# An attention and feed-forward block on one core: the first twelve tiles laid out in a new order, with finer order words

## The chip, the cores and the metric

The kernel runs on one core of a Trainium2 chip. The core has a matrix engine (PE, with its weight loads shown apart as PEld), a vector engine (DVE), a scalar engine (ACT), a general engine (POOL) and a sync engine (SP) whose queue issues every DMA of this kernel. Each engine works through its own queue in order. The metric is the device time in microseconds of one launch; the time before is 529.81 us, the median of three runs (529.16 to 530.25).

## The reference, cut to what matters

```python
# x: (4, 2048, 512), ctx: (4, 154, 512), 16 heads of 64
out = attention(layernorm(x), ctx)         # 154 keys; key j is allowed for row i when j == i
x = x + out @ Wout + bout
h = layernorm(layernorm(x)) * gamma + beta
h = qlinear(h, w1, b1); h = gelu(h); h = qlinear(h, w2, b2)
x = x + h
def qlinear(x, w, b):      # whole-number weights in -1..1, rows scaled to 127
    scale = 127 / clip(max|x| of the row, EPS); xq = round(x * scale)
    sw = 1 / clip(mean|w|, EPS);                wq = clip(round(w * sw), -1, 1)
    return xq @ wq / (scale * sw) + b
```

The first 154 rows of a batch see one key each, so their softmax is 1 and they get the projection of the key of the same number. All later rows have no allowed key, so their softmax is even and they get the mean of the 154 projected keys. So the attention is a product of the context with W = Wv Wout (the value half of Wkv), and a few added rows: the first tile of 128 rows of a batch adds 128 products, the second one adds 26 products and the mean, all others the mean alone.

## The kernel before, in words

The 8192 rows are 64 tiles of 128 rows. `seq` (L72) starts each batch with its third tile, so that the first tiles need the mean of the keys alone. Tiles are normalised in groups of 1, 1, 1, 1, 2, 2, 2, 3, 3 and then 4 (L73).

The order of the whole program is written out by hand: the scheduler is switched off, `BEGINNING` holds one word for each operation up to step U11, `STEADY` is repeated for every four tiles from tile 12 on, and `ENDING` covers the last eight. A word is a letter, a tile number and sometimes a half or an engine flag (last digit 1 for DVE, 0 for ACT or POOL). What counts for the time is how the words fall into the five queues: within one engine they keep the order of the words.

Words for the beginning: `lv`, `lo` load 128 rows of Wv and Wout, `lw i.c` loads a chunk of weight i (0 for w1, 1 for w2, eight chunks of 512 KB each), `lc` the context, `lr` a row vector spread to 128 partitions (0 bout, 1 gamma, 2 beta, 3 b2), `lb` half of b1, `L` two tiles of x. `w` adds one block to W in PSUM, `cw` copies a quarter of W out. `ms` sums |w| of a chunk, `z` makes the weight scale from the eight sums, `q` scales and rounds a chunk to int16, `c` clips it to the final f16 weight. `sk`, `mk`, `lk`, `sf` prepare key sums and means. `pm` is the product for the mean of the first batch, `pr` the one for the rest rows, `Y b` the one for the first 128 keys of batch b; `m`, `yr`, `y b` take them out of PSUM with bout added; `sr` stores the rest rows to DRAM, `s` and `t` read them back spread out.

Words for a tile: `A`/`a` add the attention rows (DVE/POOL), `S` statistics, then one of three normalisations: `O P C E` on DVE with one power on POOL (C needs the power; E needs beta), `N` with `B` (ACT normalises, POOL multiplies gamma and adds beta) or `N` with `K` (POOL does all). `R` finds the row scale, `V`/`v` the group scales, `Q` quantises (ACT), `T` transposes by DMA, `I n.h` writes b1 into a PSUM half (the seed), `U` is the up product (16 matmuls), `G` the gelu of a half, `M` the maximum of a half, `H` quantises the hidden rows, `h` transposes them by DMA, `D` is the dequantisation factor, `W` the down product, `X` adds b2, `F` finishes, `f` stores.

Resources that set the order around the change: the ring of 12 buffers for x and staged weights (a load after the twelfth waits for the release of a buffer, in the order of the words); four buffers `wi` for whole-number chunks; three PSUM pairs of banks `ps_h` (W takes two, the products of batches 0 and 1 the third; after that every half of every tile takes the one that a gelu released three halves earlier); two banks `ps_o` for the remaining products; and eight DMA semaphores used in turn, so that a DMA's issue waits for the landing of the one issued eight before it.

Lines that matter later: L203 product of ones for the weight scale, L211 and L214 quantise and clip weights, L225 absolute sum on ACT, L237 add rows, L313 the normalised row with beta (word E), L316 add b2, L336 and L338 group scales, L391 blocks of W, L402 and L404 copies of W, L420 attention products, L502/L500 seeds on ACT/DVE, L510 up, L529 gelu, L541 maximum, L563 factor D, L570 quantise hidden, L588 down, L594 finish.

Of the kernel before, what the change touches and what calls it, by code (L numbers as in the profile page):

```python
# [53 lines left out]
def xattn_ffn(ctx: ExitStack, tc, x, ctxT, WvT, Wout, bout, w1T, b1, w2T, b2, gamma, beta, out):  # L54
# [22 lines left out]
    for g, size in enumerate(sizes):  # L77
# [19 lines left out]
        G2.1 X1 S7 a8 W0 N6 R5 H1 t1 h1 M2.1 P6 V4 D2 Q4 H2 E6 T4 B7 a9
        U3 h2 a11 R6 G3.0 X2 D1 Q5 I4.0.1 S8 a10 M3.0 F0 f0 R7 T5 S9 I4.1.0 L7 G3.1 M3.1
        P8 N8
        U4 H3 a13 X3 I5.0.1 B9 L8 W1 h3 E8 S10 F1 R8 v6 G4.0 I5.1.0 f1 S11 W2 a16  # L100
        U5 G4.1 Q6 s0 I6.0.0 M4.0 G5.0 M4.1 T6 a12 F2 f2 R9 D4 H4 M5.0 h4 S12 I6.1.0 G5.1
        X4 a17 D3 M5.1 W3
        U6 L9 A14 X5 N10 F3 f3 Q7 I7.0.1 S16 a15 W4 G6.0 I7.1.0 K10 Q8 T7
        U7 H5 S17 M6.0 V8 T8 B11 a18 G6.1 S13 B12 h5 S14 Q9 M6.1 I8.0.0 D5 G7.0 I8.1.0 T9
        S15 N13 M7.0 H6 R10 G7.1 D6 K13 W5 h6 X7 R11 F4 F5 a19 f4 L10 X6
        U8 W6 I9.0.1 G8.0 M7.1 I9.1.0 R12 V10 K14 M8.0 G8.1 M8.1 f5 H7 h7 S18 Q10
        U9 I10.0.1 S19 a20 H8 G9.0 I10.1.0 G9.1 T10 M9.0 R13 F6 W7 h8 f6 Q11 M9.1 D7 L11
        B15 S20 R14 T11 P16 D8
        U10 X9 H9 G10.0 I11.0.1 M10.0 N16 h9 I11.1.0 Q12 a21 R15 F7 W8 X8
        U11 f7 G10.1 I12.0.0 a22 G11.0 M10.1 K17 D9 L12 F8 T12 H10 D10 X10 V13 S21 h10  # L110
        G11.1 I12.1.0 E16 W9 K18 M11.0 R16 a23 X11 M11.1 t2 f8 R17 F9 Q13 S22 H11 T13 h11
        f9
# [83 lines left out]
    def weight_scale(i, step=None):  # L196
        if step != 1:
            tot[i] = small.tile([P, 1], F32, tag="tot", name=f"tot_{i}")
            nc.vector.tensor_reduce(tot[i], part[i], AX.X, ALU.add)
        if step == 0:  # L200
            return
        pt = ps_o.tile([P, 512], F32, tag="po", name=f"pt_{i}")
        nc.tensor.matmul(pt[:, 0:1], ones, tot[i], start=True, stop=True)  # L203
        nc.vector.tensor_scalar(wm[i], pt[:, 0:1], 1.0 / (D * HID), EPS, ALU.mult, ALU.max)
        nc.vector.reciprocal(sw[i], wm[i])
# [523 lines left out]
```

## Time and profile before

| What | Value |
|---|---|
| median of three runs | 529.81 us |
| the profiled execution: time / span of its trace | 528.89 us / 527.1 us |
| mean granted TensorE clock | 0.992 |
| PE busy | 498.8 us, 95% of the span |
| DVE, ACT, POOL busy | 434.8, 422.4, 405.4 us |
| up products (1024 matmuls), down products (1024) | 233.5 us, 231.2 us |
| PE idle ahead of up / down products | 13.4 us / 6.0 us |
| first block of W starts / first up product starts | 4.24 us / 53.58 us |

The span is measured from the first to the last instruction of the trace, and the time adds what lies around it (1.8 us here). A matmul's recorded length contains its pipeline, so 16 matmuls that follow each other take less than 16 times the mean of one: the timeline shows one up or down product in 3.45 us. An attention product of four f32 matmuls is recorded as eight and also takes 3.45 us. DMA times are read as the time of landing. "Idle before" names what ended the wait.

### The profile page before, as it was taken

To read this page: it belongs to the slowest core of one execution; us is meant where nothing else is said; L and a number is where in the kernel's file an instruction comes from. 1 tells how busy PE (TensorE), PEld (TensorE's weight loads), DVE (VectorE), ACT (ScalarE), POOL (GpSimd) and SP (SyncE) were. 2 spreads that over 40 slices of the span, in tenths; PEclk is the share of its full clock that TensorE was granted. 3 is DMA by queue.
4 is the path that set the end of the run, shared out by engine and by line. 5 is a ranking of instruction groups with operands and counts; after the bars stand their busy time and mean duration, and the time that the engine had idled before them with its cause. 6 is when DMAs were issued, how large, how long until landed. Compare 5 with 4: busy or idle time off the path is not lost.

```text
span 527.1 us, 6898 instructions
## 1 busy us (share of the span) xinstructions
PE 498.8 (95%) x2164; PEld 222.3 (42%) x2164; DVE 434.8 (82%) x760; ACT 422.4 (80%) x387; POOL 405.4 (77%) x526
## 2 busy tenths in 40 slices
PE   6999848998999999999999999999999999999996
PEld 2444313433444444444444444444444444444442
DVE  1078998998888898989899988999999998787762
ACT  1386876698789888898888879898888888888971
POOL 0045489999999999999999999899999998852220
PEclk9999979999999999999999999999999999999999
DMA  8998066675799797868777696858596956576654
GB/s 305 401 391 304 11 174 134 182 175 141 165 188 202 140 213 157 204 156 187 164 188 167 139 234 145 193 127 206 133 207 139 218 103 158 111 168 132 130 116 125
DMA packets 194112, 94.00 MB, mean 178 GB/s; under 512 B 170268, under 2 KB 170268, under 8 KB 194076
## 3 DMA queue, kind: packets, MB, share of 16 engines
q1 hardware_dynamic: 194076, 93.56, 73.6%
q8 instruction: 17, 0.28, 0.2%
q14 instruction: 19, 0.16, 0.1%
HBM read 34.55 MB, written 17.04 MB: 98 GB/s over the span
## 4 chain that ended last, share of the span: by engine, by line
PE 57%; POOL 16%; DVE 11%; DMA 9%; ACT 3%; issue 3%; SPq 0%; ACTq 0%; POOLq 0%; DVEq 0%
PE ph L510 28%; PE po L588 27%; POOL x L237 4%; DMA xqT<-xqg 3%; DVE m L541 3%; POOL h L300 2%; POOL h L299 2%; POOL x L316 2%; DMA ctx_sb<-ctxT_dram 2%; DVE bn L244 2%; DVE ph L500 1%; DMA ws<-w2T_dram 1%; PE wps L391 1%; DVE o L594 1%; POOL r L261 1%
## 5 line engine op out<-in xcount | busy, mean ns | idle before, releaser
L510 PE MATMUL ph<-w1q,xqT 128*128 128x512 f16 x1024 | 233.5, 381 | 13.4 <-DMA xqT<-xqg 10.0
L588 PE MATMUL po<-w2q,hqT 128*128 128x512 f16 x1024 | 231.2, 379 | 6.0 <-DMA hqT<-hq 6.0
L541 DVE TENSOR_REDUCE m<-hid 128x1 f32<-128x1024 f32 (+1 forms) x130 | 152.9, 1192 | 20.4 <-ACT hid L529 19.9
L529 ACT ACTIVATE hid<-ph,d 128x1024 f32<-128x1024 f32 (+1 forms) x130 | 141.1, 1093 | 24.1 <-PE ph L510 23.2
L570 ACT ACTIVATE hq<-hid,i 128x2048 f16<-128x2048 f32 (+1 forms) x65 | 128.2, 1974 | 39.0 <-issue 19.2
L510 PEld LDWEIGHTS <-xqT 128*128 128x128 f16 x1024 | 99.9, 98 | 138.7 <-DMA xqT<-xqg 15.2
L588 PEld LDWEIGHTS <-hqT 128*128 128x128 f16 x1024 | 99.7, 98 | 128.3 <-DMA hqT<-hq 8.9
L502 ACT ACTIVATE ph<-b_b,inv 128x1024 f32<-128x1024 f32 x81 | 89.9, 1112 | 4.4 <-POOL inv L336 3.4
L316 POOL TENSOR_TENSOR x<-x,b_b 128x512 f32<-128x512 f32 x63 | 80.2, 1283 | 0.0
L299 POOL TENSOR_TENSOR h<-h,gamma_b 128x512 f32<-128x512 f32 x56 | 71.6, 1278 | 5.4 <-ACT h L287 1.2
L300 POOL TENSOR_TENSOR h<-h,beta_b 128x512 f32<-128x512 f32 x56 | 71.4, 1274 | 4.4
L237 POOL TENSOR_TENSOR x<-x,mean 128x512 f32<-128x512 f32 x55 | 69.7, 1275 | 2.8 <-DMA x<-x_dram 2.8
L594 DVE SCALAR_TENSOR_TENSOR o<-po,d,x 128x512 f32<-128x512 f32 x64 | 47.8, 746 | 16.9 <-PE po L588 8.9
L500 DVE TENSOR_SCALAR ph<-b_b,inv 128x1024 f32<-128x1024 f32 x47 | 59.6, 1268 | 1.4 <-POOL inv L336 1.3
L322 DVE TENSOR_REDUCE m<-h 128x1 f32<-128x512 f32 x64 | 43.1, 675 | 6.7 <-POOL h L300 6.6
L342 ACT ACTIVATE xqg<-h,s 128x512 f16<-128x512 f32 x64 | 45.5, 711 | 1.6 <-DVE s L330 1.6
L244 DVE BATCH_NORM_STATS2 bn<-x 128x6 f32<-128x512 f32 x64 | 43.6, 682 | 2.5 <-POOL x L237 2.4
L563 POOL TENSOR_TENSOR d<-mh,wm 128x1 f32<-128x1 f32 x64 | 12.1, 198 | 39.8 <-DVE mh L556 35.9
L294 POOL TENSOR_SCALAR h<-x,rstd,shift 128x512 f32<-128x512 f32 x50 | 38.6, 773 | 0.0
L391 PE MATMUL wps<-wo,wv 128*128 128x512 f32 x64 | 30.9, 645 | 4.2 <-DMA wo<-Wout_dram 4.2
L214 POOL TENSOR_SCALAR w1q<-wi 128x1024 f16<-128x1024 int16 x6 | 6.1, 1035 | 31.8 <-ACT wi L211 31.8
L225 ACT ACTIVATE junk<-ws 128x1024 int16<-128x1024 f32 x10 | 10.5, 1051 | 19.3 <-DMA ws<-w1T_dram 17.9
(74 smaller groups left out, 251.7 us busy)
## 6 DMA issues: line engine op xcount, KB each, us to landing
x<-x_dram SPq DMA_DIRECT2D x32, 512.0 KB, 4.9
out_dram<-o SPq DMA_DIRECT2D x64, 256.0 KB, 2.8
ws<-w1T_dram SPq DMA_DIRECT2D x8, 512.0 KB, 7.2
ws<-w2T_dram SPq DMA_DIRECT2D x8, 512.0 KB
wv<-WvT_dram SPq DMA_DIRECT2D x8, 256.0 KB, 5.9
...
hqT<-hq SPq DMA_TRANSPOSE x65, 4.3
```

The source lines that it names most:

```text
L237: e.tensor_tensor(x_of(n), x_of(n), y, ALU.add)
L244: nc.vector.bn_stats(st, x_of(n))
L299: nc.gpsimd.tensor_tensor(normed[n], normed[n], gamma_b, ALU.mult)
L300: nc.gpsimd.tensor_tensor(normed[n], normed[n], beta_b, ALU.add)
L316: e.tensor_tensor(x_of(n), x_of(n), b2_b, ALU.add)
L500: nc.vector.tensor_scalar(ph, row, d, None, ALU.mult)
L502: nc.scalar.activation(ph, row, AF.Identity, bias=0.0, scale=d)
L510: nc.tensor.matmul(bank[i], xqT[n][:, k, :], w1q[:, k, i * 512 : (i + 1) * 512], start=False, stop=(k == KD - 1), skip_group_check=True,)
L529: nc.scalar.activation(hidden[n][:, i * w : (i + 1) * w], up_ps[n][half][:, lo : lo + w], AF.Gelu, bias=0.0, scale=deq1[g][:, j : j + 1],)
L541: nc.vector.tensor_reduce(m2[:, i : i + 1], hidden[n][:, i * w : (i + 1) * w], AX.X, ALU.max, apply_absolute_value=True,)
L570: nc.scalar.activation(hq[n][:, lo : lo + w], hidden[n][:, lo : lo + w], AF.Identity, bias=0.0, scale=inv2[n],)
L588: nc.tensor.matmul(po, hqT[n][:, k, :], w2q[:, k, :], start=(k == 0), stop=(k == KH - 1))
```

## The change

It rewrites `BEGINNING`, and gives it finer words:

- **Order.** All words up to step U11 stand in a new order and partly on other engines (the last digits). `STEADY` and `ENDING` keep their order; `K` is only spelled `k e`.
- **Norm words.** `B` and `K` are split into `n` or `k` (normalise) and `e` (gamma and beta). `O` now stops before the power on POOL, which is the new word `o`.
- **Weight scale.** `z` has three words: the sum, the product of ones, the rest. `q` can run on DVE (digit 1). The absolute sum on ACT writes its unused result into the final weight's buffer instead of a `wi` buffer.
- **Attention in two parts.** `pr`, `pm`, `Y` take a range of the four contraction blocks. `sf` uses the sums of `sk` and has no sum of its own. `ctx_rest` and `sums` are kept for the whole kernel.
- **Banks.** The products of batches 0 and 1 go to `ps_o` like the others. The third pair of `ps_h` banks is taken first by two products of ones with ones (`idle`, not read by anything), then by the first seed.

The diff, cut to its core (the old order is cut after its step U2):

```diff
     BEGINNING = """
-        lv0 lo0 lv1 lv2 lo1 lo2 lw0.1 lw0.2 lw0.0 lw0.4 lo3 lv3 lo4 lv4 lo5 lv5 lw0.3 lv6
-        lo6 lv7 lw0.5 lw0.6 lw0.7 lc lw1.0 lo7 lr0 L0 lw1.2 lr2 lw1.3 lw1.4 lw1.1 lw1.5
-        lr1 lw1.6 lw1.7 lb1 L1 ms0.1.0 L2 ms0.2.1 ms0.3.0 ms0.4.0 ms0.0.1 ms0.6.0 w0 L3
-        lb0 w1 ms0.7.0 ms0.5.0 w2 w3 lr3 w4 w5 z0.0 sk0 z0.1 w6 q0.4 sk1 w7 q0.3 sf sk2
-        sk3 mk lk c0.3.1 q0.5 q0.0 c0.0.0 c0.4.0 q0.1 cw0.1 xo0 q0.2 cw1.0 c0.1.0 c0.2.0
-        cw2.0 cw3.0 pm pr ms1.0.1 q0.6 Y0.0.1 q0.7 c0.5.1 ms1.3.0 ms1.6.0 c0.6.0 ms1.2.1
-        ms1.1.1 ms1.5.1 A0 c0.7.0 S0 ms1.4.0 m Y0.1.4 O0 P0 a1 C0 E0 ms1.7.0 z1.0 R0 z1.1
-        Y2 S1 yr sr a4 q1.0 Q0 T0 q1.1 V0 O1 Y1.0.2 I0.0.0 I0.1.0 q1.2 P1 C1 a2 E1 c1.2.0
-        R1 V1 c1.1.1 Y1.2.4 S2
-        U0 q1.3 y1 Q1 T1 y0 I1.0.1 O2 end a5 c1.3.0 c1.0.1 P2 G0.0 I1.1.0 M0.0 G0.1 M0.1
-        U1 q1.5 Y3 q1.4 a3 C2 S3 O3 y2 q1.7 E2 C3 c1.7.1 P3 R2 E3 V2 G1.0 S4 q1.6 D0
-        I2.0.1 R3 c1.6.0 I2.1.0 S5 y3 c1.5.0 Q2 c1.4.0 M1.0 T2 P4 L4 V3
...
+        lv0 lo0 lo1 lo2 lv1 lw0.2 lw0.3 lw0.6 lv2 w0 lw0.0 lv3 lv4 lo3 ms0.2.1 lo4 w1
+        ms0.3.0 lw0.7 ms0.6.0 lw0.1 lo5 w2 ms0.0.1 lv5 lw0.4 lo6 lw0.5 lv6 w3 ms0.7.0 lo7
+        ms0.1.1 lv7 lc w4 lw1.4 ms0.4.0 lw1.6 L0 ms0.5.0 lr0 w5 lr1 z0.0 lw1.2 z0.1 w6
+        z0.2 q0.0.1 q0.5.0 q0.2.1 lw1.0 q0.7.0 lw1.5 sk2 c0.2.0 L1 sk3 c0.5.0 q0.4.0 sk1
+        w7 lw1.3 ms1.4.0 sk0 c0.4.0 lw1.7 c0.7.0 cw0.1 q0.1.0 sf c0.0.0 cw1.0 lw1.1 pm0.2
+        lr2 cw3.1 cw2.0 lk q0.3.0 c0.1.1 mk pm2.4 xo1 ms1.6.0 L2 q0.6.1 c0.6.1 L3 ms1.2.0
+        Y0.0.2 m lb0 A0 a1 ms1.5.0 S0 Y0.2.4 ms1.0.0 O0 P0 o0 a2 ms1.3.0 C0 pr0.2 S1
+        ms1.7.0 a3 O1 y0 ms1.1.0 c0.3.0 S2 o1 E0 a5 z1.0 R0 z1.1 z1.2 Q0 O2 Y3.0.2 P1 o2
+        q1.6.0 T0 a6 C2 q1.2.0 L4 C1 lb1 V0 lr3 q1.0.0 E1 c1.2.0 Y3.2.4 R1 I0.0.0 P2 V1
+        q1.3.0 pr2.4 a4 y3 S3 Q1 a8 I0.1.0 T1
+        U0 O3 S4 L5 L6 c1.6.0 q1.7.0 S5 o3 E2 end G0.0 c1.0.0 C3 I1.0.0 R2 a7 I1.1.0
+        U1 M0.0 V2 Q2 N4 P3 G0.1 c1.3.1 E3 q1.5.0 Y2.0.2 yr k4 q1.4.0 R3 k5 sr L7 e4 T2
+        q1.1.0 Y2.2.4 S6 I2.0.1 G1.0 Y1.0.2 c1.1.0 G1.1 S7 M0.1 V3 I2.1.0 a10
+        U2 I3.0.0 a13 M1.0 Q3 H0 M1.1 e5 T3 L8 s0 Y1.2.4 R4 G2.0 h0 N6 P6 L9 H1 A9 c1.7.1
+        c1.5.1 R5 X0 I3.1.0
+        U3 h1 t1 y1 G2.1 V4 M2.0 k7 I4.0.0 X3 S13 Q4 c1.4.0 W0 M2.1 G3.0 T4 a12 L10 G3.1
+        S8 a11 Q5 y2 I4.1.0 T5 a14 M3.0
+        U4 I5.0.0 e7 S9 H2 M3.1 W1 N8 G4.0 E6 h2 A15 G4.1 R6 R7 D0 I5.1.0 X1
+        U5 M4.0 H3 D1 k8 F0 X4 S10 n9 D2 V6 Q6 S11 e8 W2 I6.0.0 T6 F1 h3 M4.1 G5.0 f0
+        I6.1.0 X2 S12
+        U6 H4 e9 S14 R8 Q7 M5.0 G5.1 T7 X5 R9 W3 f1 h4 G6.0 D3 N10 I7.0.1 Q8 A19 I7.1.0 T8
+        M5.1 L11 V8 Q9
+        U7 k10 G6.1 T9 a16 F2 n11 I8.0.1 f2 e10 H5 F3 W4 M6.0 G7.0 h5 a20 S16 n12 a17 M6.1
+        I8.1.0
+        U8 e11 G7.1 M7.0 I9.0.0 R10 H6 e12 R11 W5 M7.1 G8.0 h6 f3 D6 x7 D7 I9.1.0 D5 a18
+        R12
+        U9 H7 S15 D4 X6 F4 Q10 S17 a21 G8.1 T10 M8.0 W6 f4 V10 h7 G9.0 X10 S20 I10.0.0
+        M8.1 N13 I10.1.0
+        U10 S18 H8 k13 F5 k15 M9.0 X8 G9.1 h8 F6 e13 W7 Q11 S19 Q12 T11 M9.1 f5 G10.0 L12
+        T12 N16 I11.0.0 f6 A22 W8 H9 x9 S21 a23 M10.0 I11.1.0 h9 D9 e15 S22 G10.1
+        U11 F7 I12.0.0 M10.1 f7 D8 G11.0 k14 e14 W9 M11.0 H10 F8 k16 R13 I12.1.0 h10 e16
+        R14 G11.1 R15 n17 M11.1 n18 e17 Q13 R16 H11 T13 F9 f8 V13 R17 f9 D10 X11 h11 t2
+        e18
     """
...
-    def quant_weight(i, c):
+    def quant_weight(i, c, vector):
         whole[i, c] = wstage.tile([P, CH], I16, tag="wi", name=f"wi_{i}_{c}")
-        nc.scalar.activation(whole[i, c], staged[i, c], AF.Identity, bias=0.0, scale=sw[i])
+        if vector:
+            nc.vector.tensor_scalar(whole[i, c], staged[i, c], sw[i], None, ALU.mult)
+        else:
+            nc.scalar.activation(whole[i, c], staged[i, c], AF.Identity, bias=0.0, scale=sw[i])
...
-            junk = wstage.tile([P, CH], I16, tag="wi", name=f"junk_{i}_{c}")
+            junk = wdst[i][:, c * CH : (c + 1) * CH]
...
     def open_norm(g):
...
+    def power_norm(g):
+        size, a, r, q = opened[g]
         nc.gpsimd.tensor_tensor(r, a, powers[:, :size], ALU.pow)
...
+    nc.gpsimd.memset(ones, 1.0)
     nc.gpsimd.memset(powers, -0.5)
...
     wps = [ps_h.tile([P, 1024], F32, tag="ph", name=f"wps_{i}") for i in range(2)]
+    idle = ps_h.tile([P, 1024], F32, tag="ph", name="idle")
+    for half in range(2):
+        nc.tensor.matmul(
+            idle[:, half * 512 : (half + 1) * 512],
+            ones,
+            ones.unsqueeze(1).to_broadcast([P, 4, P]),
+            start=True,
+            stop=True,
+        )
...
-    def rest_sum():
-        py["rest"] = ps_o.tile([P, 512], F32, tag="po", name="py_rest")
-        rows(lambda k: ctx_rest[:, k, :, :].rearrange("p b r -> p (b r)"), py["rest"])
+    def rest_sum(lo, hi):
+        if lo == 0:
+            py["rest"] = ps_o.tile([P, 512], F32, tag="po", name="py_rest")
+        lhs = ctx_rest.rearrange("p k b r -> p k (b r)")
+        rows(lambda k: lhs[:, k, :], py["rest"], range(lo, hi))
...
     def front_sum(b, lo=0, hi=KD):
-        if b < 2 and "pair" not in py:
-            py["pair"] = ps_h.tile([P, 2, D], F32, tag="ph", name="py_pair")
         if b not in py:
-            py[b] = (
-                py["pair"][:, b, :] if b < 2 else ps_o.tile([P, 512], F32, tag="po", name=f"py_{b}")
-            )
+            py[b] = ps_o.tile([P, 512], F32, tag="po", name=f"py_{b}")
         rows(lambda k: ctx_sb[:, k, b, :P], py[b], range(lo, hi))
```

More of the change, by code (lines that the diff above doesn't have):

```diff
@@ L90, in xattn_ffn @@
-        ms1.1.1 ms1.5.1 A0 c0.7.0 S0 ms1.4.0 m Y0.1.4 O0 P0 a1 C0 E0 ms1.7.0 z1.0 R0 z1.1
-        Y2 S1 yr sr a4 q1.0 Q0 T0 q1.1 V0 O1 Y1.0.2 I0.0.0 I0.1.0 q1.2 P1 C1 a2 E1 c1.2.0
-        R1 V1 c1.1.1 Y1.2.4 S2
-        U0 q1.3 y1 Q1 T1 y0 I1.0.1 O2 end a5 c1.3.0 c1.0.1 P2 G0.0 I1.1.0 M0.0 G0.1 M0.1
-        U1 q1.5 Y3 q1.4 a3 C2 S3 O3 y2 q1.7 E2 C3 c1.7.1 P3 R2 E3 V2 G1.0 S4 q1.6 D0
-        I2.0.1 R3 c1.6.0 I2.1.0 S5 y3 c1.5.0 Q2 c1.4.0 M1.0 T2 P4 L4 V3
-        U2 G1.1 a6 N4 L5 E4 H0 M1.1 a7 Q3 I3.0.0 L6 G2.0 h0 I3.1.0 T3 X0 S6 M2.0 R4 B5
@@ L97, in xattn_ffn @@
[L97 to L111, printed above, removed]
@@ L112, in xattn_ffn @@
-        f9
+        lv0 lo0 lo1 lo2 lv1 lw0.2 lw0.3 lw0.6 lv2 w0 lw0.0 lv3 lv4 lo3 ms0.2.1 lo4 w1
[4 more added lines that the diff above has]
+        lr2 cw3.1 cw2.0 lk q0.3.0 c0.1.1 mk pm2.4 xo1 ms1.6.0 L2 q0.6.1 c0.6.1 L3 ms1.2.0
@@ L115, in xattn_ffn @@
         U0 G0.0 I1.0.1 M0.0 W-2 G0.1 I1.1.0 M0.1 Q2 F-2 L14 f-2 D-1
-        U1 S11 H0 I2.0.1 G1.0 R6 T2 h0 G1.1 Q3 M1.0 X0 X1 I2.1.0 N8 W-1 K7 T3 M1.1 F-1 K8
-        H1 D0 a14 f-1
+        U1 S11 H0 I2.0.1 G1.0 R6 T2 h0 G1.1 Q3 M1.0 X0 X1 I2.1.0 N8 W-1 k7 e7 T3 M1.1 F-1
+        k8 e8 H1 D0 a14 f-1
         U2 I3.0.1 G2.0 h1 R7 M2.0 G2.1 Q4 M2.1 I3.1.0 W0 a12 L16 D2 D1 a13 R8 F0 T4 v4 S12
         H2 h2
-        U3 X2 G3.0 I4.0.0 G3.1 S13 K9 I4.1.0 W1 Q5 T5 a15 X3 M3.0 f0 M3.1 H3 K10 h3 R9 F1
-        f1 S14
+        U3 X2 G3.0 I4.0.0 G3.1 S13 k9 e9 I4.1.0 W1 Q5 T5 a15 X3 M3.0 f0 M3.1 H3 k10 e10 h3
+        R9 F1 f1 S14
     """
     ENDING = """
-        U0 G0.0 I1.0.1 W-2 M0.0 G0.1 M0.1 I1.1.0 K7 x0 Q2 F-2 H0
+        U0 G0.0 I1.0.1 W-2 M0.0 G0.1 M0.1 I1.1.0 k7 e7 x0 Q2 F-2 H0
         U1 I2.0.1 D-1 T2 G1.0 R6 M1.0 G1.1 Q3 M1.1 I2.1.0 h0 X1 f-2 W-1 T3 F-1
@@ L194, in xattn_ffn, with weight_scale @@
     tot = {}
-    def weight_scale(i, step=None):
-        if step != 1:
+    def weight_scale(i, step):
+        if step == 0:
             tot[i] = small.tile([P, 1], F32, tag="tot", name=f"tot_{i}")
             nc.vector.tensor_reduce(tot[i], part[i], AX.X, ALU.add)
[L200 to L205, printed above, removed]
+        elif step == 1:
+            py["tot", i] = ps_o.tile([P, 512], F32, tag="po", name=f"pt_{i}")
+            nc.tensor.matmul(py["tot", i][:, 0:1], ones, tot[i], start=True, stop=True)
+        else:
+            pt = py["tot", i][:, 0:1]
+            nc.vector.tensor_scalar(wm[i], pt, 1.0 / (D * HID), EPS, ALU.mult, ALU.max)
+            nc.vector.reciprocal(sw[i], wm[i])
     whole = {}
-    def quant_weight(i, c):
+    def quant_weight(i, c, vector):
         whole[i, c] = wstage.tile([P, CH], I16, tag="wi", name=f"wi_{i}_{c}")
-        nc.scalar.activation(whole[i, c], staged[i, c], AF.Identity, bias=0.0, scale=sw[i])
+        if vector:
+            nc.vector.tensor_scalar(whole[i, c], staged[i, c], sw[i], None, ALU.mult)
+        else:
+            nc.scalar.activation(whole[i, c], staged[i, c], AF.Identity, bias=0.0, scale=sw[i])
     def clip_weight(i, c, e):
@@ L380, in xattn_ffn @@
     nc.scalar.activation(warm, powers[:, 0:1], AF.Gelu)
-    nc.gpsimd.memset(ones, 1.0)
-    ctx_rest = att.tile([P, KD, B, 32], F32, tag="ctx_rest", name="ctx_rest")
+    ctx_rest = constant([P, KD, B, 32], F32, "ctx_rest")
     nc.gpsimd.memset(ctx_rest, 0.0)
-    sums = att.tile([P, KD, B], F32, tag="sums", name="sums")
+    sums = constant([P, KD, B], F32, "sums")
     wps = [ps_h.tile([P, 1024], F32, tag="ph", name=f"wps_{i}") for i in range(2)]
+    idle = ps_h.tile([P, 1024], F32, tag="ph", name="idle")
[7 more added lines that the diff above has]
+        )
     def w_block(c):
@@ L432, in xattn_ffn, with mean_rows @@
     first_mean = att.tile([P, KD, P], F32, tag="first_mean", name="first_mean")
-    first_sum = att.tile([P, KD], F32, tag="first_sum", name="first_sum")
     def spread_keys():
-        nc.vector.tensor_reduce(first_sum, ctx_sb[:, :, 0, :], AX.X, ALU.add)
         nc.vector.tensor_scalar(
-            first_mean, first_sum.unsqueeze(2).to_broadcast([P, KD, P]), 1.0 / NKV, None, ALU.mult
-        )
-    def mean_rows():
-        py["mean"] = ps_o.tile([P, 512], F32, tag="po", name="py_mean")
-        rows(lambda k: first_mean[:, k, :], py["mean"])
+            first_mean,
+            sums[:, :, 0:1].to_broadcast([P, KD, P]),
+            1.0 / NKV,
+            None,
+            ALU.mult,
+        )
+    def mean_rows(lo, hi):
+        if lo == 0:
+            py["mean"] = ps_o.tile([P, 512], F32, tag="po", name="py_mean")
+        rows(lambda k: first_mean[:, k, :], py["mean"], range(lo, hi))
     def add_bout(vector):
@@ L651, in xattn_ffn @@
         "O": on_group(open_norm),
+        "o": on_group(power_norm),
         "C": on_group(close_norm),
@@ L654, in xattn_ffn @@
         "E": close_affine,
-        "B": lambda n: (normalize(n), affine(n)),
-        "K": lambda n: (normalize_too(n), affine(n)),
+        "n": normalize,
+        "k": normalize_too,
+        "e": affine,
         "R": row_scales,
```

## The prediction

> **What bounds the kernel now.** I read the page's busy rows first, then its slices, then the PE timeline with what ended each idle time.
>
> ```profile
> PE 498.8 (95%) x2164; PEld 222.3 (42%) x2164; DVE 434.8 (82%) x760; ACT 422.4 (80%) x387; POOL 405.4 (77%) x526
> ...
> PE   6999848998999999999999999999999999999996
> ...
> POOL 0045489999999999999999999899999998852220
> ```
>
> A slice is 13.2 us. After the sixth PE is at eight or nine tenths everywhere: the 64 up and 64 down products, 128 x 3.45 us = 442 us, follow each other, so time can come only from the ends. The end (about 512 on) has the same order in both kernels. What is left is the beginning, up to U13, which starts at 159.98 in the chain of waits. POOL is half idle there and full from the seventh slice on.
>
> ```profile
> 53.58 3.62 PE L510 MATMUL ph<-w1q,xqT 128*128 128x512 f16 x16
> 58.66 3.63 PE L510 MATMUL ph<-w1q,xqT 128*128 128x512 f16 x16 [1.47 <-DMA xqT<-xqg]
> 71.33 5.42 PE L510 MATMUL ph<-w1q,xqT 128*128 128x512 f16 x16 [5.61 <-DMA xqT<-xqg]
> 79.49 3.63 PE L588 MATMUL po<-w2q,hqT 128*128 128x512 f16 x16 [2.74 <-DMA hqT<-hq]
> 88.33 3.61 PE L510 MATMUL ph<-w1q,xqT 128*128 128x512 f16 x16 [1.75 <-DVE ph L500]
> ```
>
> These are U0, U1, U2, W0, U4; the bracket is the idle time before each. Between 53.58 and 160 PE loses 1.47 + 5.61 + 2.74 + 1.75 here, 1.8 more in U2 (5.42 against 3.62), and about 4.7 in seven small gaps (the largest 1.06): 18 us. That is the most that the tiles' part of the change could bring. U2 is the largest, and its cause stands in the rows of the engines ahead of it:
>
> ```profile
> 57.70 2.55 DVE L541 TENSOR_REDUCE m<-hid 128x1 f32<-128x1024 f32 x2
> 65.29 0.68 DVE L322 TENSOR_REDUCE m<-h 128x1 f32<-128x512 f32 x1
> 66.44 0.62 POOL L336 TENSOR_TENSOR inv<-s,sw 128x1 f32<-128x1 f32 x1 [3.31 <-DVE s L330]
> 67.09 1.12 ACT L502 ACTIVATE ph<-b_b,inv 128x1024 f32<-128x1024 f32 x1 [2.94 <-POOL inv L336]
> 68.14 0.71 ACT L342 ACTIVATE xqg<-h,s 128x512 f16<-128x512 f32 x1
> ```
>
> DVE handles both maxima of tile 0 before it finishes tile 2's norm, its scale (R2) comes at 65.3, POOL and ACT wait for it, and the transpose starts behind Q2.
>
> **Part 1, the start (ones ahead of W, loads).** The first weight loads come every 0.86 us, later every 0.43 us:
>
> ```profile
> 9.49 0.34 PEld L391 LDWEIGHTS wps<-wo,wv 128*128 128x128 f32 x1 [0.52 <-issue]
> ...
> 11.11 0.19 PEld L391 LDWEIGHTS wps<-wo,wv 128*128 128x128 f32 x1 [0.24 <-issue]
> ```
>
> So PE ran at half speed from 4.24 to about 9.9, 5.7 us, and block 0 lasted until 10.86 instead of 7.7. The two products of ones are four half-speed passes of 0.85 us, from about 1.0 to 4.4, just before the first data (4.11). By this row, full speed comes 5.7 us after 1.0, at 6.7: block 0 ends at 8.9. [...] Either way block 2 waits for `wv2`, now ninth in the load order: the landing records pass 256 KB in 0.66 us and 512 KB in 1.33 us, so it lands at about 12.1. W ends at 12.2 + 6 x 3.45 = 33.0 against 35.05. [...]
>
> The first weight scale: the last chunk of w1 lands at 23.3 (24.5 before), the sum is ready at 24.7, but its product of ones stands behind block 5 (26.1): scale at 26.8 against 28.75. Three chunks quantised on DVE: the trace has no such form; bounds are 0.42 (the clip, L214, 1024 int16) and 1.27 (the seed, L500, 1024 f32); nearest is `first_mean` (L438), f32 in SBUF, 0.43 for 512, so 0.7 each. Key sums 4 x 0.7 follow the context (28.5, before 27.7), so `first_mean` is ready at 32.2 and the mean product ends at 36.5 (38.7 before). Dropping the separate sum and the `wi` buffers of ACT's sums costs nothing; they only remove 0.7 us of DVE and a wait.
>
> **Part 2, to the first up product.** From the mean: A0, S0, P0, power, C0 end at 40.4. Then DVE takes S1, O1, y0, S2 (2.3 us) ahead of E0, which was next to C0 before. E0 also needs beta, moved from the 30th load to the 38th: 15.7 MB are ahead of its end, and before the same bytes had landed at 43.7. So E0 starts at 43.8, not 44.38, and R0 ends at 46.0 (46.5 before). Q0 stands first on ACT now (46.0; before 47.89, behind a chunk of w2): transpose lands at 50.0 against 51.88.
>
> PE in the meantime: Y0 and half of `pr` end at 41.7, then the second product of ones waits for the sum of w2 (last chunk lands 43.1, ready 44.9) and Y3 for the bank that `z1.2` frees (46.3). This is a new hole of 4.6 us. [...] It is covered: Y3 and the rest of `pr` (5.2 us) end at 51.5 to 53.3, U0 needs its seeds (ACT: Q0, three chunks of w2, seed 50.9; one more chunk, Q1, second seed 53.6). U0 ends at 55.4 (57.2 before).
>
> **Part 3, U1 to W0.** ACT is the path: G0.0, both seeds of tile 1, to 57.8; U1 ends at 60.2. Then Y2 and half of Y1 (5.2 us) stand where PE idled: to 65.4. R2 is at 56.3 (DVE, one maximum or none ahead of it), Q2 at 57.8; the transpose waits on SP behind the store of the rest rows, which waits for `yr` (DVE, after E3, 59.7), and a load of x: issued 60.6, landing near 64. Behind it are T3 and h0 only, needed later. Seed I2.1 comes at 65.6. **U2 starts at 65.5 instead of 71.33.** T3 is issued at 67.3, lands near 70 for U3 at 70.7; the second seed of tile 3 stands behind H0, G2.0, H1 on ACT (73.1): 0.7 us of wait. The last clip of w2 stands on POOL behind N6, X0, V4, k7, X3 and ends at 78.3: W0 waits there and ends at 80.0. The same set of products (U0 to U3, W0, all Y) ended at 86.5 before: 6.5 us. U4 then has its seed and goes on at once: 8.3 us.
>
> **Part 4, U4 to U13.** Per-engine sums with 0.61 a Q, 1.05 a seed or chunk, 1.0 a gelu, 1.9 an H: ACT has 87.5 us of work from Q0 to G11.1 (five seeds moved from DVE to ACT, +5.3); my walk ends it at 138.7, 92.7 us after 46.0. POOL: three more tiles with gamma and beta (2.6 each) and four more with its own normalise (0.85), three row additions and two X less (1.23 each): +5 us, but it starts earlier, and adding its rows with no idle gives V10 119.6, e14 139.6, V13 146. PE reaches U13 at 145.8 and waits for V13's seed: 147.5. No data are late on SP. Before, U13 began at 160.0: **12.5 us**. The walk counts no delay between engines. ACT is 94% busy in it, against this row:
>
> ```profile
> 53.58:160.00 106.42, 90.17 (x394) 38.85 (x393) 95.96 (x182) 85.19 (x79) 93.23 (x137) 0.97 0.63 147
> ```
>
> There (PE, PEld, DVE, ACT, POOL) ACT was busy 80% and POOL 88%. At 90% for ACT, which is the middle of 94 and 86, the walk is 4.5 us longer, of which PE feels what its lead (some 1 us at U10) does not cover: I take 3.5. The gain is 9 us. From U13 on PE is the bound as before and keeps it; the small gaps after 160 (0.75, 0.88, 0.97, 0.21) come from unchanged words.
>
> **Sum.** The profiled execution took 528.89 (span 527.1); minus 9 gives 519.9. The median of the runs is 0.9 above that execution: **520.8**.
>
> **Rivals.**
> 1. *POOL or ACT becomes the bound from U4 on*, so that only the hole at U2 and the start are won. For it: POOL's slices are full from the seventh on and it gets 5 us more. Against: it is idle for half or more of slices 3 to 5 and starts earlier. What stays is 4 to 6 us: 525.
> 2. *Slower: ACT's fixed queue.* The walk has ACT at 94%; before, it idled 106.4 - 85.2 = 21.2 us between 53.6 and 160. If the same idle falls into the new order, ACT ends 87.5 + 21.2 = 108.7 after 46.0, at 154.7 instead of 138.7, so U13 moves by 16, to 163.5: 3.5 us behind before, 533. It decides from 12.5 us of added ACT idle on. For it: seeds and quantisations stand behind each other there, and one late scale from POOL holds all. Against: much of that idle was waiting for PE and for late scales, which come earlier now.
> 3. *The order does not do what it says*: beta or the last chunks land so late, or SP blocks so (store of the rest rows ahead of T2), that U2 stays near 71; then 0 to 1 us: 529.5.
>
> **Chances.** Forecast 0.55, rival 1 0.21, rival 2 0.18, rival 3 0.06. The unknown costs: DVE chunks 0.42 to 1.27 (-0.8 to +1.7 us, covered by the wait for beta), the clock in the hole 0 to 1.8 (covered up to 1.5), delays between engines 0 to 7. The forecast alone spans 516 to 524; with rival 1 and the start of rival 2 it is 515.5 to 529. Differences under 0.2%, 1.06 us, can't be told from none. Faster 0.77, same 0.05, slower 0.18.
>
> **What would show it.** Right: block 0 of W ends near 9; a PE hole of 4 to 5 us before Y3, ended by `wm` of w2; U0 at 51 to 53, U2 at 65 to 67, W0 held at its ninth matmul by POOL; U13 near 151. Wrong: U2 later than 69, PE idle of several us ahead of U5 to U12 ended by seeds of ACT or scales of POOL, or PE slow for more than 4 us after the hole.

## The result and the profile after

The changed kernel took 524.77 us (median of four runs, 523.67 to 525.33) where the kernel before took 529.68 us on the same chip (529.16 to 530.25). The ratio is 0.9904, with a 95% interval of 0.9884 to 0.9925: **faster by 4.9 us**. The forecast was 520.8, so about half of the 9 us it promised arrived. The profiled execution took 525.17 us with a span of 523.2, so between the two profiled executions the gain is 3.9 us of span; the numbers below are of these two.

The busy row and two of the slices of the page:

```profile
PE 501.1 (96%) x2168; PEld 223.8 (43%) x2168; DVE 433.2 (83%) x753; ACT 426.3 (81%) x393; POOL 410.5 (78%) x532
...
PE   8997987999999989999999989999999899999996
...
POOL 0048999999999999899999898999999998852220
```

POOL, half idle in slices 3 to 5 before, is at eight tenths in the fourth and full from the fifth on. PE's sixth slice, the hole ahead of U2, rose from 4 to 8. But behind the beginning PE has three new dips from 9 to 8, the fifteenth, the 24th and the 32nd slice of 13.1 us each, which begin at 183, 301 and 405 us: they return below.

The PE timeline up to U4 (start, length, operation, matmuls; in the bracket the idle time before it and what ended it):

```profile
0.97 3.52 PE L405 MATMUL idle<-ones 128*128 128x512 f32 x4 [0.97 <-POOL powers L390]
12.83 14.00 PE L415 MATMUL wps<-wo,wv 128*128 128x512 f32 x32 [1.47 <-DMA wv<-WvT_dram]
...
45.67 0.59 PE L206 MATMUL pt<-tot,ones 128*128 128x1 f32 x2 [3.17 <-DVE tot L203]
46.77 6.23 PE L444 MATMUL py<-w_sb,ctx_sb 128*128 128x512 f32 x8 [0.50 <-DVE wm L209]
...
54.55 3.62 PE L534 MATMUL ph<-w1q,xqT 128*128 128x512 f16 x16
...
67.30 3.62 PE L534 MATMUL ph<-w1q,xqT 128*128 128x512 f16 x16
...
76.03 1.89 PE L534 MATMUL ph<-w1q,xqT 128*128 128x512 f16 x8 [1.57 <-ACT ph L526]
...
81.44 1.89 PE L612 MATMUL po<-w2q,hqT 128*128 128x512 f16 x8 [0.67 <-POOL w2q L222]
85.72 5.31 PE L534 MATMUL ph<-w1q,xqT 128*128 128x512 f16 x16 [2.39 <-DMA xqT<-xqg]
```

From above: the ones, W's third block on, the weight scale of w2, Y3, then U0, U2, the second half of U3, the second half of W0, and U4. U2 starts 4.0 us earlier than before (67.30 against 71.33). U4 stands at 85.72 against 88.33. Between W1 (90.87) and 160 no gap in PE is listed at all. U13 starts at 153.03 where the same timeline of the kernel before has 159.81 (the 159.98 of the prediction is from the chain of waits, which counts from the end of the product ahead): **6.8 us ahead**. But the span ends only 3.9 us earlier. What the timeline of the changed kernel lists from U13 on, and then that of the kernel before:

```profile
153.03 3.62 PE L534 MATMUL ph<-w1q,xqT 128*128 128x512 f16 x16
...
190.10 3.63 PE L534 MATMUL ph<-w1q,xqT 128*128 128x512 f16 x16 [2.06 <-DMA xqT<-xqg]
273.60 3.63 PE L534 MATMUL ph<-w1q,xqT 128*128 128x512 f16 x16 [0.45 <-DMA xqT<-xqg]
302.73 3.63 PE L534 MATMUL ph<-w1q,xqT 128*128 128x512 f16 x16 [1.33 <-DMA xqT<-xqg]
415.03 3.63 PE L534 MATMUL ph<-w1q,xqT 128*128 128x512 f16 x16 [1.62 <-DMA xqT<-xqg]
```

```profile
159.81 3.62 PE L510 MATMUL ph<-w1q,xqT 128*128 128x512 f16 x16
...
167.64 3.63 PE L510 MATMUL ph<-w1q,xqT 128*128 128x512 f16 x16 [0.75 <-DMA xqT<-xqg]
...
196.32 3.63 PE L510 MATMUL ph<-w1q,xqT 128*128 128x512 f16 x16 [0.88 <-DMA xqT<-xqg]
...
307.96 3.63 PE L510 MATMUL ph<-w1q,xqT 128*128 128x512 f16 x16 [0.97 <-DMA xqT<-xqg]
...
418.86 3.63 PE L510 MATMUL ph<-w1q,xqT 128*128 128x512 f16 x16 [0.21 <-DMA xqT<-xqg]
```

Three of the waits answer to the 0.88, 0.97 and 0.21 of before, the one at 273.60 is new, and the 0.75 is gone. The words there are the same in both kernels, yet the four waits have grown from 2.8 to 5.5 us. That is nearly all of the 2.9 us by which the lead shrinks.

### The profile page after: what moved, and what is told of

Same layout as the page of the kernel before. It is cut to its first block, busy times and chain, and to the rows that moved or that the text cites. A ratio compares the mean times of both kernels' runs of the same rounds, so it can differ in the third digit from the quotient of the medians.

```text
span 523.2 us, 6893 instructions
## 1 busy us (share of the span) xinstructions
PE 501.1 (96%) x2168; PEld 223.8 (43%) x2168; DVE 433.2 (83%) x753; ACT 426.3 (81%) x393; POOL 410.5 (78%) x532
## 4 chain that ended last, share of the span: by engine, by line
PE 57%; POOL 18%; DMA 10%; DVE 6%; ACT 4%; issue 3%; SPq 1%; DVEq 0%; ACTq 0%; POOLq 0%
PE ph L534 27%; PE po L612 26%; DMA xqT<-xqg 6%; PE wps L415 4%; POOL x L246 4%; POOL h L312 3%; POOL h L311 3%; DVE m L565 2%; POOL x L328 2%; DMA x<-x_dram 2%; ACT hq L594 2%; DMA wv<-WvT_dram 2%; POOL h L306 1%; POOL r L270 1%; ACT hid L553 1%
## 5 line engine op out<-in xcount | busy, mean ns | idle before, releaser
L526 ACT ACTIVATE ph<-b_b,inv 128x1024 f32<-128x1024 f32 x86 | 95.3, 1112 | 3.2 <-POOL inv L348 2.1
L312 POOL TENSOR_TENSOR h<-h,beta_b 128x512 f32<-128x512 f32 x59 | 75.6, 1282 | 4.6
L311 POOL TENSOR_TENSOR h<-h,gamma_b 128x512 f32<-128x512 f32 x59 | 75.0, 1271 | 3.9
L328 POOL TENSOR_TENSOR x<-x,b_b 128x512 f32<-128x512 f32 x61 | 77.0, 1272 | 0.0
L246 POOL TENSOR_TENSOR x<-x,mean 128x512 f32<-128x512 f32 x52 | 65.7, 1273 | 5.0 <-DVE mean L661 3.8
L524 DVE TENSOR_SCALAR ph<-b_b,inv 128x1024 f32<-128x1024 f32 x42 | 53.2, 1267 | 0.6 <-ACT hid L553 0.6
L306 POOL TENSOR_SCALAR h<-x,rstd,shift 128x512 f32<-128x512 f32 x54 | 41.9, 776 | 0.2
L415 PE MATMUL wps<-wo,wv 128*128 128x512 f32 x64 | 28.1, 595 | 1.5 <-DMA wv<-WvT_dram 1.5
L415 PEld LDWEIGHTS wps<-wo,wv 128*128 128x128 f32 x64 | 11.9, 190 | 17.3 <-issue 13.9
```

Of the source, the lines that this page charges most:

```text
L246: e.tensor_tensor(x_of(n), x_of(n), y, ALU.add)
L311: nc.gpsimd.tensor_tensor(normed[n], normed[n], gamma_b, ALU.mult)
L312: nc.gpsimd.tensor_tensor(normed[n], normed[n], beta_b, ALU.add)
L328: e.tensor_tensor(x_of(n), x_of(n), b2_b, ALU.add)
L415: nc.tensor.matmul(wps[k // 2][:, (k % 2) * 512 : (k % 2 + 1) * 512], wv[c][:, k * P : (k + 1) * P], wo[c], start=(c == 0), stop=(c == KI ...
L524: nc.vector.tensor_scalar(ph, row, d, None, ALU.mult)
```

## The experiments

Two questions: what gave the lead back after 160, and why U13 came at 153 and not at 151 (or at 147.5, as the walk without an allowance had it). Each kernel ran beside the kernel before on the same chip; after_no_spread and before_no_spread ran on another chip than the rest. A trace shows one execution, so a reading of stalls is of that one alone.

**late_ones.** The two products of ones are moved from ahead of W into the hole of PE before the weight scale of w2.

```diff
-    for half in range(2):
-        nc.tensor.matmul(idle[:, half * 512 : (half + 1) * 512], ones, ...)
...
         rows(lambda k: lhs[:, k, :], py["rest"], range(lo, hi))
+        for half in range(2 if lo == 0 else 0):
+            nc.tensor.matmul(idle[:, half * 512 : (half + 1) * 512], ones, ...)
```

> The two products of ones are moved from ahead of W to behind the first half of the rest rows, into the hole of PE. Theory 1 (the warm start is covered by the loads and by beta, the cold Y3 is not): W starts at half speed again, its first block ends near 10.9 and W near 35.1 (33.8 after the change), the mean row is 1.3 later, of which 0.7 is covered by the wait for beta; Y3 runs in 3.5 instead of 6.2 and the first up product starts at 52 to 53 instead of 54.6. Total within 1 us of the changed kernel (523.5 to 525.5). Rival (the warm start is worth its 2.8 us on the path): 526.5 to 528.

524.37 us (523.86 to 524.87), ratio 0.9909 [0.9885, 0.9933]. W's blocks are at full speed only from about 10 us on (the trace has 3 of their matmuls from 8 to 10 us and 6 from 10 to 12), W ends 1.0 us later (34.78 against 33.76), and it doesn't matter: U0 starts at 54.12 against 54.55. The products ahead of W bring nothing to the total, as expected. But the run changes two things, since the ones now stand in the hole, and there the expectation missed: Y3 stayed slow (5.40 us, not 3.5, at a mean granted clock of 0.57 from 47 to 50 us), although the ones ended only 0.83 us before the scale's product, and U0 did not come at 52 to 53.

**warm_hole.** Three more products of ones in the hole, in the bank of the scale's product, just ahead of it.

```diff
             py["tot", i] = ps_o.tile([P, 512], F32, tag="po", name=f"pt_{i}")
+            if i == 1:
+                for _ in range(3):
+                    nc.tensor.matmul(py["tot", i], ones, ones.unsqueeze(1).to_broadcast([P, 4, P]), ...)
```

> Three more products of ones stand in the hole of PE, just ahead of the one for the scale of w2, and nothing else is changed. Theory 1 (the hole of 3.2 us lets the clock fall, and that pushes the first up product behind its seeds): Y3 in 3.5 instead of 6.2 us, first up product at 51.6 to 52 instead of 54.55; its second half then waits for the seed behind the second half of b1 (55.2), so U0 ends near 57 instead of 58.1; total 0.5 to 1.5 us less than the changed kernel if the lead survives, 0 if a later bound takes it. Rival (Y3 is slow for its operands or banks): Y3 stays near 6.2.

524.47 us (523.65 to 524.87), ratio 0.9912 [0.9891, 0.9934]: no difference from the changed kernel. In its PE timeline (Y3, the two halves of U0, U1):

```profile
46.91 3.70 PE L453 MATMUL py<-w_sb,ctx_sb 128*128 128x512 f32 x8 [0.30 <-DVE wm L218]
...
52.16 1.89 PE L543 MATMUL ph<-w1q,xqT 128*128 128x512 f16 x8
55.33 1.89 PE L543 MATMUL ph<-w1q,xqT 128*128 128x512 f16 x8 [1.28 <-ACT ph L535]
58.41 3.61 PE L543 MATMUL ph<-w1q,xqT 128*128 128x512 f16 x16 [1.19 <-ACT ph L535]
```

Y3 takes 3.70 us instead of 6.23 and U0 begins 2.4 us earlier, but its second half waits for the seed of ACT, and U1 gains 0.3 us. The slow clock in the hole is real (granted 0.50 from 47 to 50 us in the changed kernel, 1.00 here), and from U1 on it is hidden, as the prediction had it.

**turns_first.** On SP the loads and spreads L8, s0, L9, t1, L10 are issued behind the transposes T4 and T5 instead of ahead of them.

```diff
-U2 ... T3 L8 s0 Y1.2.4 ... P6 L9 H1 A9 c1.7.1
+U2 ... T3 Y1.2.4 ... P6 H1 A9 c1.7.1
-U3 h1 t1 y1 ... T4 a12 L10 G3.1 ... T5 a14 M3.0
+U3 h1 y1 ... T4 L8 s0 a12 G3.1 ... T5 L9 t1 L10 a14 M3.0
```

> On SP the loads L8, L9, L10 and the spreads s0, t1 are moved behind the transposes T4 and T5, so that h0, h1, T4 follow T3 at once. Theory 1 (SP's queue and the filled DMA rings make T4 late): hqT0 lands near 76 instead of 78.8, T4 is issued at 80 instead of 81.9 and lands near 82.5 instead of 85.7, U4 starts at 83 to 83.6 instead of 85.72 and runs at full speed (3.6 instead of 5.3). Theory 2, on what follows: POOL is on the chain from 106 to 176, so that a lead of 2.5 to 4 us at U4 is mostly gone at the stall before the up product that began at 190.1: total 0 to 1.5 us less. Rival: nothing takes the lead, total 2.5 to 4 us less than the changed kernel.

524.47 us (524.28 to 524.59), ratio 0.9914 [0.9894, 0.9933]. U4 does start earlier, at 83.48 and at full speed (3.62 us, granted clock 1.00 from 82 to 88), so that W1 is 3.9 us ahead of the changed kernel (86.94 against 90.87). But almost nothing of it is left at U13 (152.75 against 153.03). The lead goes in small stalls:

```profile
81.76 1.89 PE L612 MATMUL po<-w2q,hqT 128*128 128x512 f16 x8 [1.78 <-POOL w2q L222]
94.76 3.63 PE L612 MATMUL po<-w2q,hqT 128*128 128x512 f16 x16 [0.75 <-DMA hqT<-hq]
...
141.96 3.63 PE L612 MATMUL po<-w2q,hqT 128*128 128x512 f16 x16 [0.99 <-DMA hqT<-hq]
```

(Two more, at 123.08 and 133.90, are of 0.52 and 0.30 us.) So at U13 something other than PE is as late as PE. Its POOL is busy as much in each stretch as the changed kernel's (19.18 of 20 us from 80 to 100, 19.02 from 100 to 120).

**no_x.** The ten additions of b2 on POOL in the beginning are left out.

```diff
-        c1.5.1 R5 X0 I3.1.0
-        U3 h1 t1 y1 G2.1 V4 M2.0 k7 I4.0.0 X3 S13 Q4 ...
+        c1.5.1 R5 I3.1.0
+        U3 h1 t1 y1 G2.1 V4 M2.0 k7 I4.0.0 S13 Q4 ...
...
```

> The changed kernel without the ten additions of b2 on POOL in the beginning (words X for the tiles 0 to 6, 8, 10, 11), 12 us of POOL; these tiles lack b2 in the output. Theory A (POOL's backlog makes PE give back its lead behind U13): the stall of 2.1 us at 190 goes, and the total is 2 to 4 us less than the changed kernel. Theory B (the spread of the next batch's rows and a load and a store ahead of the transpose make it): stalls at 190, 302 and 415 stay within 0.5 of 2.1, 1.3, 1.6, total within 1 us of the changed kernel, apart from what the lighter POOL gives at W0 and U4 (up to 1.5).

524.34 us (521.75 to 525.25), ratio 0.9904 [0.9869, 0.9938]. Neither theory is met: in the trace the wait at 190 shrinks to 0.33 us and the one at 302 to 0.73, the one at 415 stays (1.57), the one at 273 grows (0.87), one of 0.66 at 162 is new, and the total did not fall by A's 2 to 4 us. The trace is of one of the slower of the four executions (525.17 us) and its PE came later, with U2 at 68.70 and U13 at 154.48. So a backlog of POOL isn't shown to give the lead back, but this run alone doesn't rule it out.

**after_no_spread and before_no_spread.** The words `s` and `t` of the steady part, which read the rest rows back from DRAM spread over 128 partitions, are left out of the changed kernel and of the kernel before. There are four places: `s` at the end of three blocks and `t` at the end of one. In the changed kernel SP issues them at 180.61, 265.24, 292.89 and 405.51, each time just ahead of one of the four waits.

```diff
-    second = [constant([P, D], F32, f"second{b}") for b in range(2)] * 2
+    second = [constant([P, D], F32, "second0")] * B
...
         do_all(STEADY, n)
-        if n % TB == 12:
-            do(f"s{n // TB + 1}")
-        if n % TB == 8 and n // TB + 2 < B:
-            do(f"t{n // TB + 2}")
```

> The changed kernel without the spreads of rest rows and mean in the steady part (words s and t there; one tile holds the second rows of all batches), so that the rows of later batches get wrong attention rows. Theory B (the spread ahead of the transpose makes the stalls at the batch ends, and PE's lead over the other engines is given back there): the stalls at 190, 302 and 415 (2.1, 1.3, 1.6) fall below 0.3 each and the total is 4 to 6 us less than the changed kernel. Theory A (POOL's backlog): the stall at 190 stays above 1.5, the total is less by 0 to 2.

> The same left out of the kernel before. Theory B: its stalls at 196, 308 and 419 (0.9, 1.0, 0.2) go, total 1.5 to 2.5 us less than before, so that the difference between the two kernels without spreads is 6.5 to 7.5 us, what stood at U13, instead of 4.9. Theory A: less by 0 to 1, difference between the two still 4 to 5.

520.24 us (519.48 to 521.4), ratio 0.9829 [0.9808, 0.9851], and 526.88 us (526.76 to 527.54), ratio 0.9948 [0.9918, 0.9977]. Between the two there are now 6.6 us, as expected and close to the 6.8 us of U13's lead. All four waits are gone; what the timeline of after_no_spread lists behind 150 is this:

```profile
160.16 3.63 PE L534 MATMUL ph<-w1q,xqT 128*128 128x512 f16 x16 [0.20 <-DMA xqT<-xqg]
509.46 3.63 PE L612 MATMUL po<-w2q,hqT 128*128 128x512 f16 x16 [0.34 <-DMA hqT<-hq]
```

So the spreads cost the changed kernel about 4.5 us and the kernel before 2.6 to 2.8 (2.6 against the 529.48 us that it took on this chip; the changed kernel did not run there). How they do it is in SP's rows of the changed kernel, here ahead of the up product at 190 (start, time for the issue, operation):

```profile
180.61 0.41 SPq L493 DMA_DIRECT2D second<-rest_dram  x1
181.07 0.32 SPq L496 DMA_DIRECT2D second<-rest_dram  x1
181.49 0.40 SPq L176 DMA_DIRECT2D x<-x_dram  x1
183.01 0.36 SPq L623 DMA_DIRECT2D out_dram<-o  x1
183.48 1.70 SPq L365 DMA_TRANSPOSE xqT<-xqg  x1
```

and in its chain of waits (start, length, what):

```profile
183.48 6.58 DMA xqT<-xqg
190.10 3.63 PE ph L534 x16
```

When the transpose is issued, the two reads of `s` (26 rest rows, and the mean spread to 102 partitions), a load of two tiles and a store stand just ahead of it in the DMA queue, and it takes 6.58 us. The one issued at 203.77, with none of them ahead of it, lands in 2.4.

**moved_spread and before_moved_spread.** Nothing is left out: `s` and `t` are issued behind h2 of the same block, where the next transpose has some 6 us to spare.

```diff
-        do_all(STEADY, n)
+        early, late = STEADY.split("h2", 1)
+        do_all(early + "h2", n)
         if n % TB == 12:
             do(f"s{n // TB + 1}")
         if n % TB == 8 and n // TB + 2 < B:
             do(f"t{n // TB + 2}")
+        do_all(late, n)
```

> The changed kernel, with the words s and t of the steady part issued after h2 of the same block (two tiles earlier in the order) instead of at the block's end, ahead of L14, f-2 and T2. Nothing is left out. Theory 1 (the lead is given back because the spread rows stand on SP and on the DMA engines just ahead of T2 of the next block, the transpose with the least slack; T5 behind the new place has some 6 us): the gaps ahead of the up products near 190, 273, 302 and 415 us go, as in after_no_spread, and the time is 520 to 521.5 us. Rival (the 257 KB of a spread cost the DMA engines the same wherever they stand): the gaps only move, the time stays within 523.5 to 525.

> The same move of s and t in the kernel before. Theory 1: its gaps at 196, 308 and 419 us go, as in before_no_spread: 526.5 to 527.5 us, and so 6 to 7 us between this kernel and moved_spread, the lead that the changed kernel has at U13. Rival: 529 to 530.

519.63 us (519.18 to 520.68), ratio 0.9808 [0.9785, 0.9832], and 527.14 us (526.28 to 527.54), ratio 0.9945 [0.9926, 0.9964]. The first is a little under the expected 520 to 521.5, the second as expected. The same bytes cost nothing there: both are level with the kernels that don't move them at all. The two versions differ by 7.5 us, a little over the expected 6 to 7. Two of SP's rows of moved_spread around the same place, the end of the spread and the transpose:

```profile
173.33 0.28 SPq L496 DMA_DIRECT2D second<-rest_dram  x1
...
183.84 1.22 SPq L365 DMA_TRANSPOSE xqT<-xqg  x1
```

The transpose at 183.84 is issued no earlier than the one at 183.48 above, but its product starts at 188.08 with no wait, against 190.10. PE was free for it at the same time in both (190.10 less 2.06 is 188.04). The load and the store still stand just ahead of the transpose (issued at 181.03 and 183.40). So neither SP's time nor a backlog of another engine makes the wait at this place, but the spread ahead of the transpose in the DMA queue.

**turns_no_x.** turns_first and no_x in one, to see whether POOL ate the lead of turns_first.

> turns_first and no_x in one: the transposes T4 and T5 ahead of the loads and spreads on SP, and the ten additions of b2 on POOL left out in the beginning (those tiles lack b2 in the output). Theory (POOL's queue is what ate the lead of turns_first between U4 and U13: its busy time per stretch is the same in turns_first as in the changed kernel, 19.2 of 20 us from 80 to 100): with 11 us less on POOL the stalls ahead of the down products at 95, 123, 134 and 142 go and U13 comes 67.3 to 67.8 us after U4 (69.3 in turns_first, 67.3 in the changed kernel), near 151. Rival (ACT's fixed queue sets it): 68.7 us or more after U4, stalls at the same places. The total says little here, since the gaps at 190 and 303 us stay.

521.99 us (521.33 to 524.26), ratio 0.9858 [0.983, 0.9885]. The trace is of the slowest of the four executions (524.26; the others took 521.33 to 522.15), so its stalls need not stand in those. In it U13 comes 70.7 us after U4 (152.37 and 81.70), which the theory missed and the rival allows, but not with the rival's stalls: those at 123, 134 and 142 are gone, as the theory has it, and the one at 95 grew, for another reason than POOL:

```profile
95.42 5.31 PE L611 MATMUL po<-w2q,hqT 128*128 128x512 f16 x16 [3.06 <-DMA hqT<-hq]
```

Its chain shows `hqT` under way for 7.18 us, from an issue at 88.19, with the spread t1 (84.36) and the load L10 (87.67) just ahead of it: the mechanism of the spreads once more. So in this execution relief of POOL removes the stalls between, and the lead then goes to a transpose behind a spread. The expectation held that the total would say little; yet the median is 2.5 us under that of turns_first, where no_x alone gained 0.4 on the changed kernel. That fits two limits that each hide the relief of the other, though these kernels were not all measured side by side.

**combined.** moved_spread, warm_hole and turns_first in one.

> moved_spread, warm_hole and turns_first in one; nothing is left out. Theory (POOL sets U13 at 152.6 to 153 whatever the lead at U4 is): U4 near 83, U13 at 152.4 to 152.8 again, and the time that of moved_spread within 0.5 us. Rival (the leads add up): U13 near 150.5 and 1.5 to 2.5 us less than moved_spread.

518.83 us (518.46 to 519.66), ratio 0.9794 [0.9771, 0.9817]. U13 is at 152.84, as the theory says, so the leads don't add up before it; the time is 0.8 us less than that of moved_spread, a little more than the 0.5 allowed, but the runs of the two overlap.

**clip_and_t1 and x_on_dve.** In the first, built on combined, the last clip of w2 goes to DVE, t1 and L10 stand behind h2 and t2 behind h9. In the second, the additions of b2 of tiles 5, 6 and 8 go to DVE too.

```diff
-c1.4.0 W0 ... T5 L9 t1 L10 a14 M3.0 ... h2 A15 G4.1 ... T6 F1 ... h11 t2
+c1.4.1 W0 ... T5 L9 a14 M3.0 ... h2 t1 L10 G4.1 ... T6 A15 F1 ... h9 t2 D9 ... h11
```

```diff
-T7 X5 R9 ... D4 X6 F4 ... M9.0 X8 G9.1
+T7 x5 R9 ... D4 x6 F4 ... M9.0 x8 G9.1
```

> combined, with the last clip of w2 (c1.4) on DVE instead of POOL, t1 and L10 issued behind h2 instead of ahead of it (and A15, which reads s0's rows, two tiles later), and t2 issued behind h9 instead of after h11. Nothing is left out. In turns_no_x the one long stall (3.06 us ahead of the down product at 95 us) was h2 landing 7.2 us after its issue, with t1 and L10 just ahead of it. Theory (from U4 to U13 POOL's queue sets the pace; a transpose behind a spread is late): no stall inside W0 near 81.8, U4 near 81.7, none of over 0.3 us at 95, and POOL's 1.04 us less lets U13 come at 151.6 to 152.2 (152.84 in combined); time 518.0 to 518.6. Rival (U13 is held by something that is not POOL, as ACT's queue): U13 stays at 152.6 to 153, time 518.8.

> clip_and_t1, with the additions of b2 for tiles 5, 6 and 8 on DVE (0.69 us each by its rows of add) instead of POOL (1.25 us each). Nothing is left out. Theory: 3.75 us less in POOL's queue, of which U13 gains 1 to 2 us on clip_and_t1 until DVE (18.5 of 20 us busy from 120 to 140, and 2.1 us more of it now) or ACT is the next bound: U13 at 150 to 151, time 516.5 to 517.8. Rival (ACT's queue sets U13, or DVE is already as full as POOL): U13 within 0.4 us of clip_and_t1 or later, and the time the same or above.

518.86 us (518.64 to 519.26), ratio 0.9794 [0.9764, 0.9824], and 517.74 us (517.3 to 518.37), ratio 0.9772 [0.9742, 0.9802]. The stalls inside W0 and at 95 are gone in clip_and_t1, though U4 waits 1.16 us for its transpose now (83.42 instead of 81.7), and U13 stays at 153.00: the theory's 151.6 to 152.2 missed and the rival's 152.6 to 153 came. Yet POOL's queue has no idle stretch here either. What it was relieved of came back: its 13 additions of beta took 1.34 us each (1.32 in combined), its nine normalisations 0.80 (0.77), its 11 factors D 0.27 (0.23), and from 54.6 us to U13 it is busy 93.02 us against 92.86. So this run doesn't tell POOL from the rival's ACT. In x_on_dve U13 comes at 152.23, 0.8 us earlier for three additions less on POOL (3.8 us), less than the 1 to 2 expected. On DVE the three took 1.65, 0.97 and at least 1.37 us instead of the 0.69 assumed, and DVE was busy 19.52 of 20 us from 120 to 140. POOL now idles once, waiting for the statistics of DVE, and the chain of waits leaves it from 91 to 133 for DVE, ACT and a transpose:

```profile
132.82 0.20 POOL L278 TENSOR_SCALAR a<-mv 128x4 f32<-128x4 f32 x1 [2.12 <-DVE mv L263]
```

Its runs lie under all those of clip_and_t1. **x_on_dve is the fastest version, 12 us under the kernel before.**

## Why the prediction was half right

**Start.** Block 0 was to end at 8.9, with full speed from 6.7 on. W's matmuls run at full speed from 4.33 on, 3.4 us after the ones began and not the 5.7 that I took from the row: their weight loads come every 0.43 us from 4.76 to 6.91, where those of the kernel before come every 0.86 us up to 9.49. (The granted clock reads 1.00 in these microseconds in both kernels; the speed is read from the spacing of the matmuls.) Block 2 waits for `wv2` as forecast (landing some 0.7 us later), and W ends at 33.76 instead of 33.0. DVE's chunks took 0.70 us each, as taken. None of it reached U0, as late_ones shows.

**First up product.** E0 started at 44.80 instead of 43.8, because beta landed later, and the hole is there with the cause that was named. The slow clock cost Y3 2.6 us (6.23 against 3.60; granted 0.50 from 46 to 51 us), more than the 0 to 1.8 that the chances had for the hole. That is what put U0 at 54.55 instead of 51 to 53: in warm_hole it starts at 52.16. "It is covered" holds only from U1 on, since the total of warm_hole didn't move.

**U1 to W0.** The order of causes was right: U2 at 67.30 (65.5 forecast), the second half of U3 held by ACT's seed (1.57 us), W0 held at its ninth matmul by the last clip on POOL, at 81.4 instead of 78.3. Then the first wrong step: "U4 then has its seed and goes on at once". It had the seed but not the transpose. T4 was issued at 81.87 behind the loads and spreads and the transposes of hidden rows on SP, and U4 waited 2.39 us and then took 1.7 us longer (5.31 against 3.62, at a granted clock of 0.50 from 86 to 89 us). "No data are late on SP" was wrong, by about 4 us at W1 (turns_first).

**U4 to U13.** The step that failed in size is POOL's sum. It had V10 at 119.6 and V13 at 146; the trace has them at 123.2 and 150.4, with no idle stretch between. Of the 4.4 us at V13, 3.1 stood already at the end of the last clip of w2, 81.4 instead of 78.3, and POOL has no idle stretch from 52 us on. Its rows (the last clip, V10, V13):

```profile
80.34 1.05 POOL L222 TENSOR_SCALAR w2q<-wi 128x1024 f16<-128x1024 int16 x1
...
123.15 0.19 POOL L348 TENSOR_TENSOR inv<-s,sw 128x3 f32<-128x3 f32 x1
...
150.36 0.19 POOL L348 TENSOR_TENSOR inv<-s,sw 128x3 f32<-128x3 f32 x1
```

The rest of the way to U13 is a maximum and a seed on DVE (2.0 us in the chain of waits of combined, 150.81 to 152.84), so POOL alone would put U13 at about 152.5. ACT is busy in 88.62 of 98.48 us from U0 to U13, the 90% that was taken, and POOL in 93.10, or 95%. PE without stalls, from its late U4, also arrives at 153. So the lead was limited twice, and no cure of one side moved U13: turns_first freed PE, clip_and_t1 took 1 us from POOL, and it stayed at 152.7 to 153.0. This is rival 1 in part. It isn't POOL alone: x_on_dve took 3.8 us from it and won 0.8. Rival 1's 525 us is nearly the time that was measured, but in part by luck: it expected 4 to 6 us that last, and the kernel had 6.8 at U13 and lost 2.9 behind it.

**After U13.** "PE is the bound as before and keeps it; the small gaps after 160 (...) come from unchanged words" is the step that cost most: 2.9 us of the lead were lost there. Unchanged words don't make an unchanged wait. With the spreads moved or left out, the lead stays (7.5 and 6.6 us). Why the same spreads cost the changed kernel 1.7 us more is settled in part. The chain of waits of the kernel before has at the first place:

```profile
191.25 5.02 DMA xqT<-xqg
196.32 3.63 PE ph L510 x16
```

PE was free for this product 4.2 us after the issue of the transpose (196.32 less 0.88, less 191.25), in the changed kernel 4.6 us. At the places of the other two `s`, worked out in the same way from the issues in the two chains (301.54 and 413.02, 295.77 and 407.79), it is 5.45 and 5.63 us in the kernel before and 5.63 and 5.62 in the changed one. So PE hadn't run ahead of the transposes. They took longer: 6.58, 6.91 and 7.20 us against 5.02, 6.38 and 5.79. Why the same bytes took longer is open.

In all, between the two profiled executions: 5 us too much, 2 of them ahead of U13 (153.0 against 151) and the rest behind it. By the medians it is 4.
